# Three rearrangements in a fused two-layer kernel: combinations of B^T, two intermediates of a convolution, and column sums of W

## The chip, the cores and the metric

One core of a Trainium2 chip runs the kernel. The metric is the device time of one execution in microseconds (us). The core has five engines with a queue of their own each: TensorE (PE, matmuls), VectorE (DVE), ScalarE (ACT), GpSimd (POOL) and SyncE (SP, which here only issues transfers). An engine executes its own queue in order, and waits for the others where data or a buffer asks for it.

## The reference

All data is float32: x is 32 x 128 x 2048. Two residual layers follow each other:

```python
# layer 0: a mixture of 8 1x1 convolutions per batch entry (attention from cond), then a linear layer with 16 LoRA-like updates
att = softmax(mlp(cond));  agg_w = einsum('bk,koi->boi', att, weight);  agg_b = att @ bias_k
y = einsum('boi,bih->boh', agg_w, x) + agg_b[:, :, None]
x = x + y @ W.T + bias + sum_e coeffs[e]*scales[e] * (y @ A[e].T) @ Bf[e].T
# layer 1: a grouped 9-tap convolution along h with a context bias, then 16 small FFNs on permuted columns
z = conv1d(x, weight, groups=4) + ctx + bias
x = x + unpermute(down(gelu(up(permute(z)))))
```

The kernel folds A, B, coeffs and scales into one matrix W' = W^T + A^T B^T of 2048 x 2048, multiplies x by W' first, and mixes the channels with agg_w afterwards. The bias agg_b then appears as agg_b times the sum of each column of W'. Those 2048 column sums are called w1.

## The kernel before, in words

**Making W' and multiplying.** W' is made in 16 blocks of 128 partitions x 2048 columns (`blocks`, 4 groups of 4 kc). The first four blocks are made by `w_make` (L162): for each of four quarters, two matmuls of A^T and B^T into a PSUM bank (L172), and a DVE addition of the bank to W (L176). The other twelve are made two at a time by `w_make_two` (L205), which uses a seven-product scheme of the Strassen kind: it needs combinations of A (`a_combine`) and of B^T (`b_combine`, L193). The products are P1, P2, P6, P5, P7, P3, P4, and each is read from its bank by DVE (L213). P1, P6, P7, P4 accumulate in the same banks, so P6 can start only when DVE has read P1. `b_combine(1, ...)` runs on DVE at L873, between the first four blocks and the first `w_make_two`; `b_combine(0, ...)` runs on POOL at L912.

The large product x W' is again a seven-product scheme, two levels deep. The outer level are seven rounds (`ROUNDS`), each with eight steps g, so 56 steps i of some 24 us. Each step is a `multiply` (L316) of seven products P1, P2, P6, P5, P7, P3, P4 (L332, 4 matmuls of 128x512 each, which are 8 records), whose banks DVE or ACT adds to accumulators (L325, L327). After the first six products `between(j)`, j = 0 to 5, puts other work into the queues. POOL combines x (`x_combine`, L296 to L299) and the weights (`inner_weights`, L239 to L243) one step or round ahead.

**Buffers.** Nearly all SBUF tiles are 8 KB per partition and come from one pool of 24 slots (`slot`). A tile asks for a slot at its first use and gives it back after its last. The engine's queue waits if none is free.

**The small chain.** `small()` (L715) is a generator that is advanced once at the end of each step (L960). Steps 0 to 4 make attention weights and context biases. At step 5, when all 16 blocks are made, it makes w1: `wsum`, in which DVE and POOL have added up the blocks (128 partitions x 2048), is multiplied by a 128 x 128 matrix of ones (L801), so that each partition has the sum over all partitions; ACT copies the banks to `wbc` (L804) and SP stores the 128 x 2048 result in `w1_d` (L806). Steps 6 to 12 transform the convolution's Toeplitz weights (tiles `tw`, `t1`, L810 to L831) and store them. In the last round `late_loads` (L705) loads them and w1; `mix_begin` (L429) uses w1 on ACT.

**Last round and FFN stage.** In the last round (steps 48 to 55) and in the 128 heads of the FFN loop (L971), a pipeline over 16 pairs c of batch entries is threaded between the matmuls. Its places n go from -2 to 9; place n of pair c stands at k = 8c - 21 + n, where k < 0 are thirds of the steps of the last round and k >= 0 are heads. At each k there are three calls: `stage_first`, `stage_second` and `stage_third`. Between second and third stand one or two products of the round, or the down product of a head. The convolution is done by a scheme with six inner products per half i (i = 0 at places 4 to 6, i = 1 at places 7 to 9): `conv_inputs` (L494) makes v1 to v4 (`va`, L514, L517, L516, L518, in the code `v[0]`, `v[1]`, `v[2]`, `v[3]`) and v0, v5 (`vb`, L521 to L525) on DVE; `conv_begin` multiplies v1 and v3 at place 5 or 8, `conv_middle` v2 and v4 at place 6 or 9, `conv_end` v0 and v5. `oes`, the even and odd parts from which v1 to v4 come, live in the room of v0 and v5 in `vb`. `residual_rows` (L481) transposes the residual x in 32x32 blocks on DVE, after `conv_inputs` at places 4 and 5.

The order within a queue is that of the program text; nothing reorders it.

Of the kernel before, what the change touches and what calls it, by code (L numbers as in the profile page):

```python
# [16 lines left out]
P = 128  # L17
# [34 lines left out]
def adaln_ffn_kernel(  # L52
# [32 lines left out]
    def done(*ps):  # L85
        banks.extend(ps)
# [8 lines left out]
        for kh in range(2) for oh in range(2) for kc in range(4)  # L95
    }
    t2_d = {kc: scratch(f"t2_d{kc}") for kc in range(4)}
    w1_d = scratch("w1_d")
    tw_d = scratch("tw_d")
    te_d = scratch("te_d", (P, KEXP * P))  # L100
    ag_d = [scratch(f"ag_d{i}") for i in range(B // NCH)]
# [57 lines left out]
    def w_store(k, t):  # L159
        nc.gpsimd.dma_start(wb_d[k], t.rearrange("p k o c -> p (k o c)"))  # L160

    def w_make(k, t):  # L162

        kh, oh, kc = k
        for oi in range(2):
            for ki in range(2):
                pw = bank()

                n = QW // 2 if k == (0, 0, 0) and oi == 0 else QW
                for o0 in range(0, QW, n):  # L170
                    for c in range(2):
                        nc.tensor.matmul(  # L172
                            pw[:, o0 : o0 + n], lhsT=a_sb[kh][:, c, ki, kc],
                            rhs=bf_sb[oh][:, c, oi, o0 : o0 + n], start=(c == 0), stop=(c == 1),
                        )
                nc.vector.tensor_tensor(t[:, ki, oi], pw, t[:, ki, oi], ALU.add)  # L176
                done(pw)
        w_store(k, t)


# [12 lines left out]
    def b_combine(oh, tt):  # L193
        t = slot(f"tb_{oh}", (P, 4, QW))
        b11, b12, b21, b22 = (bf_sb[oh][:, c, oi] for c in range(2) for oi in range(2))
        tt(t[:, 0], b12, b11, ALU.subtract)
        tt(t[:, 1], b22, t[:, 0], ALU.subtract)
        tt(t[:, 2], b22, b12, ALU.subtract)
        tt(t[:, 3], b21, t[:, 1], ALU.subtract)
        return {  # L200
            "P1": b11, "P2": b21, "P3": b22, "P4": t[:, 3],
            "P5": t[:, 0], "P6": t[:, 1], "P7": t[:, 2],
        }
# [290 lines left out]
    def conv_inputs(c, i, part):  # L494
# [4 lines left out]
        low, high = xg[:, :, 0 : 2 * NM], xg[:, :, 2 * NM : 4 * NM]  # L499
        if i == 0 and part == 0:  # L500
            vb[c] = slot(f"vb_{c}", (P, 2, 2, 4 * NM))
        if part == 0:
            va[c, i] = slot(f"va_{c}{i}", (P, 4, 4 * NM))
            v = [va[c, i][:, q].rearrange("p (r m) -> p r m", r=4) for q in range(4)]

            oes = [
                vb[c][:, h].rearrange("p q (r m) -> p (q r m)", r=4).rearrange(
                    "p (r k m) -> p r (k m)", r=4, k=2
                )
                for h in (1 - i, i)  # L510
            ]
            (o0, e0), (o1, e1) = ((t[:, :, 0:NM], t[:, :, NM : 2 * NM]) for t in oes)
            stt(oes[0], low, -4.0, high, ALU.mult, ALU.add)  # L513
            tt(v[0], e0, o0, ALU.add)  # L514
            tt(oes[1], high, low, ALU.subtract)  # L515
            stt(v[2], o1, 2.0, e1, ALU.mult, ALU.add)  # L516
            tt(v[1], e0, o0, ALU.subtract)  # L517
            stt(v[3], o1, -2.0, e1, ALU.mult, ALU.add)  # L518
        else:
            v0, v5 = (vb[c][:, i, q].rearrange("p (r m) -> p r m", r=4) for q in range(2))  # L520
            stt(v0, d[1], -5.0, d[3], ALU.mult, ALU.add)  # L521
            stt(v5, d[2], -1.25, d[0], ALU.mult, ALU.add)
            w0, w5 = v0[:, :, 1:NM], v5[:, :, 0 : NM - 1]
            stt(w0, d[3][:, :, 0 : NM - 1], 4.0, w0, ALU.mult, ALU.add)
            stt(w5, d[0][:, :, 1:NM], 0.25, w5, ALU.mult, ALU.add)  # L525
# [89 lines left out]
    def stage_second(c, n):  # L615
        if n in (6, 9):
            conv_middle(c, int(n == 9))
        if n in (0, 2):
            mix_begin(2 * c + n // 2)

# [12 lines left out]
    def third_rest(c, n):  # L633
# [3 lines left out]
            residual_rows(c, 0, 0)  # L637
            residual_rows(c, 0, 1)
        if n in (4, 5, 7, 8):
            conv_inputs(c, int(n > 5), n in (5, 8))  # L640
        if n in (4, 5):
            residual_rows(c, 1, n - 4)
        if n == 8:
# [61 lines left out]
    def late_loads():  # L705
        late["tw"] = slot("tw_l", (P, 4, GR, P))
        nc.sync.dma_start(late["tw"].rearrange("p k r c -> p (k r c)"), tw_d)
        late["w1"] = slot("w1", (P, NPH, QW))
        nc.sync.dma_start(late["w1"].rearrange("p f n -> p (f n)"), w1_d)
        late["fb"] = slot("fb", (P, NPH, QW))  # L710
        nc.sync.dma_start(
            late["fb"].rearrange("p f n -> p (f n)"), fbias.to_broadcast([P, L])
# [3 lines left out]
    def small():  # L716
# [77 lines left out]

        while len(made) < 16:
            yield
        wbc = slot("wbc", (P, NPH, QW))
        for o in range(NPH):
            p5 = bank()
            for half in (slice(0, NQ), slice(NQ, QW)):  # L800
                nc.tensor.matmul(  # L801
                    p5[:, half], lhsT=ones, rhs=wsum[:, o // 2, o % 2, half], start=True, stop=True
                )
            nc.scalar.copy(wbc[:, o], p5)  # L804
            done(p5)
        nc.sync.dma_start(w1_d, wbc.rearrange("p f n -> p (f n)"))  # L806
        yield


# [51 lines left out]
    sa[0] = a_combine(0, nc.gpsimd.tensor_tensor)  # L861
    first = [wt.pop(k) for k in blocks[0:4]]

    def make_first(kc):
        t = first[kc]
        w_make(blocks[kc], t)
        made.append(blocks[kc])
        if kc == 2:
            lhs[0] = x_combine(*steps[0], xs.pop(0))
        nc.gpsimd.tensor_tensor(wsum[:, 0, 1], wsum[:, 0, 1], t[:, 0, 1], ALU.add)  # L870

    rhs = inner_weights("P1", first, make_first)
    tb[1] = b_combine(1, nc.vector.tensor_tensor)  # L873
    a_load(1, 0, 4)
    unsummed, unsummed_first = [], list(first)
    olds = {}
# [8 lines left out]
    for i, (r, g) in enumerate(steps):  # L885
# [16 lines left out]
        if ri == 0:  # L902
            ks = blocks[4 + 2 * g : 6 + 2 * g]
            if ks:
# [4 lines left out]
                    a_scale(1, 0, 4)  # L909
                    sa[1] = a_combine(1, nc.gpsimd.tensor_tensor)  # L910
                if g == 3:
                    tb[0] = b_combine(0, nc.gpsimd.tensor_tensor)  # L912
                for k, t in zip(ks, two):
                    unsummed.append((k[1], t))
                    if k[:2] == (1, 0):
# [137 lines left out]
```

## Time and profile before

| what | value |
|---|---|
| runs, median (lowest to highest) | 2639.94 us (2638.82 to 2642.12), 3 runs |
| the profiled execution | 2637.23 us, span 2635.5 us |
| granted TensorE clock, mean | 0.998 |
| L332 matmuls, seven rounds | 3136 records, 592 ns each |
| L676 and L687, FFN products | 1024 records each, 592 ns each |
| L406, mixed kernels on DVE | 158.9 us |
| L427, bias on POOL | 178.9 us |
| DMA | 609.18 MB, mean 231 GB/s |

The span is the time from the first to the last instruction that the profile shows; 1.7 us of the execution lie around it. In a timeline each line has the start, the length, the engine, the line of the code, the operation, the tiles out<-in, their shapes and the count of merged instructions; in brackets is the idle time before it and what ended it. In the list of waits stand the total, the number and the longest. A matmul of float32 shows as two records.

### The profile page before, as it was taken

How to read it: one execution, taken by the hardware profiler on the slowest of the kernel's cores; microseconds unless marked ns; L12 is line 12 of the kernel's file. 1: busy time of each engine (PE TensorE's matmuls, PEld its weight loads, DVE VectorE, ACT ScalarE, POOL GpSimd, SP SyncE). 2: the span in 40 equal slices, each digit the busy share in tenths (PEclk: the TensorE clock that was granted, in tenths of full speed). 3: DMA queues.
4: the chain of work that ended last, by engine and by line, in shares of the span. 5: the costliest groups of instructions: out<-in, count | busy, mean ns of one | idle time of the engine just before them, and what ended most of it. 6: DMA issues, size and time to landing. Idle time of an engine off the chain costs nothing.

```text
span 2635.5 us, 20243 instructions
## 1 busy us (share of the span) xinstructions
PE 2614.5 (99%) x6484; PEld 1230.3 (47%) x6484; DVE 1336.4 (51%) x2168; ACT 535.3 (20%) x1103; POOL 1230.7 (47%) x1014
## 2 busy tenths in 40 slices
PE   9999999999999999999999999999999999999998
PEld 4444444444444444444444445555455555455543
DVE  5554134344233454433366666766666666666610
ACT  0000000000000000000011144444444444444432
POOL 7321536878746644756332334434443344344222
PEclk9999999999999999999999999999999999999999
DMA  8542458788466577555667798777778777777532
GB/s 319 206 160 105 162 193 325 271 319 352 155 258 255 203 285 309 223 230 206 223 229 239 227 317 282 236 221 229 227 244 257 234 222 224 240 242 240 166 123 88
DMA packets 183610, 609.18 MB, mean 231 GB/s; under 512 B 16849, under 2 KB 88017, under 8 KB 139089
## 3 DMA queue, kind: packets, MB, share of 16 engines
q1 hardware_dynamic: 150080, 474.79, 50.6%
q0 software_dynamic: 32992, 132.14, 14.8%
q8 instruction: 52, 0.85, 0.1%
q10 hardware_dynamic: 432, 0.96, 0.1%
q14 instruction: 54, 0.43, 0.0%
HBM read 372.42 MB, written 201.85 MB: 218 GB/s over the span
## 4 chain that ended last, share of the span: by engine, by line
PE 96%; DVE 2%; DMA 1%; issue 0%; SPq 0%; POOLq 0%; ACT 0%; DVEq 0%; ACTq 0%
PE bank L332 50%; PE bank L676 16%; PE bank L687 16%; PE bank L534 6%; PE bank L442 4%; PE bank L210 2%; PE bank L172 1%; DMA xg<-x 1%; DMA ws<-in_ffw 0%; DVE vb L515 0%; DMA a_sb<-in_A 0%; DVE vb L513 0%; DVE va L514 0%; PE bank L801 0%; DVE va L516 0%
## 5 line engine op out<-in xcount | busy, mean ns | idle before, releaser
L676 PE MATMUL bank<-t,ws 128*128 128x512 f32 x1024 | 460.7, 592 | 0.6 <-DMA ws<-in_ffw 0.4
L687 PE MATMUL bank<-gl,ws 128*128 128x512 f32 x1024 | 460.2, 592 | 0.0
L694 POOL DMA_INDIRECT out<-t,orow x128 | 151.1, 1180 | 532.7 <-DVE t L692 458.6
L325 DVE TENSOR_TENSOR u<-bank,u 128x512 f32<-128x512 f32 x280 | 187.6, 688 | 415.4 <-PE bank L332 405.7
L679 ACT ACTIVATE gl<-bank 128x512 f32<-128x512 f32 x512 | 306.1, 598 | 446.4 <-PE bank L676 436.0
L332 PE MATMUL bank<-P_t,s_P 128*128 128x512 f32 x896 | 393.7, 592 | 0.0
L687 PEld LDWEIGHTS bank<-gl,ws 128*128 128x128 f32 x1024 | 194.6, 190 | 233.0 <-issue 231.5
L676 PEld LDWEIGHTS bank<-t,ws 128*128 128x128 f32 x1024 | 194.4, 190 | 227.8 <-issue 223.5
L332 PE MATMUL bank<-wo_P,s_P 128*128 128x512 f32 x640 | 281.6, 592 | 3.1 <-DVE u L325 3.1
L427 POOL TENSOR_TENSOR x<-x,fb 128x512 f32<-128x512 f32 x128 | 178.9, 1427 | 223.9 <-DMA x<-in_x 223.9
L332 PE MATMUL bank<-wo_P,xt 128*128 128x512 f32 x640 | 281.5, 592 | 0.0
L332 PEld LDWEIGHTS bank<-P_t,s_P 128*128 128x128 f32 x896 | 170.2, 190 | 213.4 <-issue 212.1
L433 ACT ACTIVATE bank<-w,aggb 128x512 f32<-128x512 f32 x128 | 80.8, 683 | 890.3 <-DVE ags L406 872.8
L692 DVE TENSOR_TENSOR t<-bank,t 128x512 f32<-128x512 f32 x128 | 88.3, 690 | 321.3 <-PE bank L687 307.7
L269 POOL TENSOR_TENSOR xt<-xt,xt 128x512 f32<-128x512 f32 x128 | 159.9, 1283 | 157.5 <-DMA xt<-in_xT 157.5
L332 PE MATMUL bank<-P_t,xt 128*128 128x512 f32 x448 | 201.4, 592 | 0.0
L325 DVE TENSOR_TENSOR p<-bank,p 128x512 f32<-128x512 f32 x112 | 77.5, 692 | 235.3 <-PE bank L332 232.1
L296 POOL TENSOR_TENSOR s_P<-xt 128x512 f32<-128x512 f32 x56 | 71.9, 1285 | 264.5 <-DMA xt<-in_xT 208.4
L332 PEld LDWEIGHTS bank<-wo_P,s_P 128*128 128x128 f32 x640 | 121.5, 190 | 155.3 <-issue 153.5
L332 PEld LDWEIGHTS bank<-wo_P,xt 128*128 128x128 f32 x640 | 121.6, 190 | 152.2 <-issue 150.2
L406 DVE SCALAR_TENSOR_TENSOR ags<-mix,att_bc,ags 128x128 f32<-128x128 f32 x224 | 158.9, 709 | 4.5
L660 POOL DMA_INDIRECT t<-hx_d,row x128 | 132.3, 1034 | 57.2 <-issue 26.0
(144 smaller groups left out, 2643.8 us busy)
## 6 DMA issues: line engine op xcount, KB each, us to landing
xt<-in_xT SPq DMA_DIRECT2D x88, 1024.0 KB
u<-u_d SPq DMA_DIRECT2D x40, 1024.0 KB
wo_P<-wb_d SPq DMA_DIRECT2D x36, 1024.0 KB
u<-c_d SPq DMA_DIRECT2D x64, 512.0 KB
x<-in_x SPq DMA_DIRECT2D x32, 1024.0 KB
xg<-x SPq DMA_DIRECT2D x256, 128.0 KB
hx_d<-x1t SPq DMA_DIRECT2D x32, 1024.0 KB
hx_d<-ht SPq DMA_DIRECT2D x32, 1024.0 KB
```

Source lines behind the costliest of these rows:

```text
L269: nc.gpsimd.tensor_tensor(out[:, i, j], a[:, i, j], b[:, i, j], op)
L325: nc.vector.tensor_tensor(to, ps, to, ALU.add)
L332: nc.tensor.matmul(ps, lhsT=lhs[k][:, bass.ts(kc, P)], rhs=rhs[k][kc], start=first and kc == 0, stop=last and kc == 3, skip_group_check=True,)
L406: nc.vector.scalar_tensor_tensor(ag, mix[:, k], att, ag, ALU.mult, ALU.add)
L427: nc.gpsimd.tensor_tensor(xt[:, f], xt[:, f], late["fb"][:, f], ALU.add)
L442: nc.tensor.matmul(pm, lhsT=ag, rhs=u[:, f], start=False, stop=True, skip_group_check=True)
L534: nc.tensor.matmul(out, lhsT=w[:, 2 * i + r], rhs=rhs, start=first and r == 0, stop=last and r == 1, skip_group_check=True,)
L660: nc.gpsimd.indirect_dma_start(out=t.rearrange("p k t -> p (k t)"), out_offset=None, in_=hx_d[g].rearrange("l k t -> l (k t)"), in_offset= ...
L676: nc.tensor.matmul(pu, lhsT=w[:, m * P : (m + 1) * P], rhs=t[:, 0], start=True, stop=True)
L679: nc.scalar.activation(gl[m], pu, AF.Gelu)
L687: nc.tensor.matmul(pd, lhsT=w[:, (MC + m) * P : (MC + m + 1) * P], rhs=gl[m], start=(m == 0), stop=(m == MC - 1),)
L694: nc.gpsimd.indirect_dma_start(out=out, out_offset=bass.IndirectOffsetOnAxis(ap=orow[:, g, h : h + 1], axis=0), in_=t[:, 1], in_offset=None,)
```

## The change

Three things are changed. (1) `conv_inputs` has three parts in place of two: v2 and v4 are made by a part of their own, which `stage_second` calls at places 5 and 8, where before they followed v3 at places 4 and 7. (2) `b_combine` returns a function that makes one of its four combinations for each call; `w_make` calls it after each of the four additions of the block kc = 3, and the call at L873 goes. On POOL, at L912, all four are still made together. (3) The products of `wsum` with ones, the ACT copies and the store of 128 equal rows go. In their place DVE transposes `wsum` in blocks of 32x32 and adds up each block's rows (128 x 64 numbers), a transfer stores them, a second one reads them back with the four groups of 32 partitions side by side in 32 partitions, DVE adds up the four and transposes, and a third transfer stores w1 as one row of 2048. These five pieces are separated by steps of the small chain, which has four steps more. `late_loads` reads w1 with a broadcast to 128 partitions. The transfers are issued from ACT's queue.

```diff
--- before.py
+++ after.py
@@ -95,7 +95,8 @@
         for kh in range(2) for oh in range(2) for kc in range(4)
     }
     t2_d = {kc: scratch(f"t2_d{kc}") for kc in range(4)}
-    w1_d = scratch("w1_d")
+    w1_d = scratch("w1_d", (1, L))
+    red_d = scratch("red_d", (P, L // GC))
     tw_d = scratch("tw_d")
     te_d = scratch("te_d", (P, KEXP * P))
     ag_d = [scratch(f"ag_d{i}") for i in range(B // NCH)]
@@ -159,7 +160,7 @@
     def w_store(k, t):
         nc.gpsimd.dma_start(wb_d[k], t.rearrange("p k o c -> p (k o c)"))
 
-    def w_make(k, t):
+    def w_make(k, t, between=lambda: None):
 
         kh, oh, kc = k
         for oi in range(2):
@@ -175,6 +176,7 @@
                         )
                 nc.vector.tensor_tensor(t[:, ki, oi], pw, t[:, ki, oi], ALU.add)
                 done(pw)
+                between()
         w_store(k, t)
 
 
@@ -193,11 +195,15 @@
     def b_combine(oh, tt):
         t = slot(f"tb_{oh}", (P, 4, QW))
         b11, b12, b21, b22 = (bf_sb[oh][:, c, oi] for c in range(2) for oi in range(2))
-        tt(t[:, 0], b12, b11, ALU.subtract)
-        tt(t[:, 1], b22, t[:, 0], ALU.subtract)
-        tt(t[:, 2], b22, b12, ALU.subtract)
-        tt(t[:, 3], b21, t[:, 1], ALU.subtract)
-        return {
+        parts = [
+            (t[:, 0], b12, b11), (t[:, 1], b22, t[:, 0]), (t[:, 2], b22, b12), (t[:, 3], b21, t[:, 1])
+        ]
+
+        def part():
+            if parts:
+                tt(*parts.pop(0), ALU.subtract)
+
+        return part, {
             "P1": b11, "P2": b21, "P3": b22, "P4": t[:, 3],
             "P5": t[:, 0], "P6": t[:, 1], "P7": t[:, 2],
         }
@@ -499,8 +505,9 @@
         low, high = xg[:, :, 0 : 2 * NM], xg[:, :, 2 * NM : 4 * NM]
         if i == 0 and part == 0:
             vb[c] = slot(f"vb_{c}", (P, 2, 2, 4 * NM))
-        if part == 0:
-            va[c, i] = slot(f"va_{c}{i}", (P, 4, 4 * NM))
+        if part < 2:
+            if part == 0:
+                va[c, i] = slot(f"va_{c}{i}", (P, 4, 4 * NM))
             v = [va[c, i][:, q].rearrange("p (r m) -> p r m", r=4) for q in range(4)]
 
             oes = [
@@ -510,12 +517,14 @@
                 for h in (1 - i, i)
             ]
             (o0, e0), (o1, e1) = ((t[:, :, 0:NM], t[:, :, NM : 2 * NM]) for t in oes)
-            stt(oes[0], low, -4.0, high, ALU.mult, ALU.add)
-            tt(v[0], e0, o0, ALU.add)
-            tt(oes[1], high, low, ALU.subtract)
-            stt(v[2], o1, 2.0, e1, ALU.mult, ALU.add)
-            tt(v[1], e0, o0, ALU.subtract)
-            stt(v[3], o1, -2.0, e1, ALU.mult, ALU.add)
+            if part == 0:
+                stt(oes[0], low, -4.0, high, ALU.mult, ALU.add)
+                tt(v[0], e0, o0, ALU.add)
+                tt(oes[1], high, low, ALU.subtract)
+                stt(v[2], o1, 2.0, e1, ALU.mult, ALU.add)
+            else:
+                tt(v[1], e0, o0, ALU.subtract)
+                stt(v[3], o1, -2.0, e1, ALU.mult, ALU.add)
         else:
             v0, v5 = (vb[c][:, i, q].rearrange("p (r m) -> p r m", r=4) for q in range(2))
             stt(v0, d[1], -5.0, d[3], ALU.mult, ALU.add)
@@ -615,6 +624,8 @@
     def stage_second(c, n):
         if n in (6, 9):
             conv_middle(c, int(n == 9))
+        if n in (5, 8):
+            conv_inputs(c, int(n == 8), 1)
         if n in (0, 2):
             mix_begin(2 * c + n // 2)
 
@@ -637,7 +648,7 @@
             residual_rows(c, 0, 0)
             residual_rows(c, 0, 1)
         if n in (4, 5, 7, 8):
-            conv_inputs(c, int(n > 5), n in (5, 8))
+            conv_inputs(c, int(n > 5), 2 * (n in (5, 8)))
         if n in (4, 5):
             residual_rows(c, 1, n - 4)
         if n == 8:
@@ -706,7 +717,7 @@
         late["tw"] = slot("tw_l", (P, 4, GR, P))
         nc.sync.dma_start(late["tw"].rearrange("p k r c -> p (k r c)"), tw_d)
         late["w1"] = slot("w1", (P, NPH, QW))
-        nc.sync.dma_start(late["w1"].rearrange("p f n -> p (f n)"), w1_d)
+        nc.sync.dma_start(late["w1"].rearrange("p f n -> p (f n)"), w1_d.to_broadcast([P, L]))
         late["fb"] = slot("fb", (P, NPH, QW))
         nc.sync.dma_start(
             late["fb"].rearrange("p f n -> p (f n)"), fbias.to_broadcast([P, L])
@@ -794,16 +805,27 @@
 
         while len(made) < 16:
             yield
-        wbc = slot("wbc", (P, NPH, QW))
+
+        wsq = slot("wsq", (P, NPH, 16, GC))
+        red, four = take(P, 4 * 16), take(GC, 4 * 4 * 16)
+        col, line = take(GC, 4 * 16), take(GC, 4 * 16)
         for o in range(NPH):
-            p5 = bank()
-            for half in (slice(0, NQ), slice(NQ, QW)):
-                nc.tensor.matmul(
-                    p5[:, half], lhsT=ones, rhs=wsum[:, o // 2, o % 2, half], start=True, stop=True
-                )
-            nc.scalar.copy(wbc[:, o], p5)
-            done(p5)
-        nc.sync.dma_start(w1_d, wbc.rearrange("p f n -> p (f n)"))
+            nc.vector.transpose(wsq[:, o].rearrange("p j c -> p (j c)"), wsum[:, o // 2, o % 2])
+            nc.vector.tensor_reduce(red[:, o * 16 : (o + 1) * 16], wsq[:, o], AX.X, ALU.add)
+        yield
+        nc.scalar.dma_start(red_d, red)
+        yield
+        nc.scalar.dma_start(
+            four.rearrange("c (g j) -> c g j", g=4), red_d.rearrange("(g c) j -> c g j", g=4)
+        )
+        yield
+        nc.vector.tensor_reduce(col, four.rearrange("c (g j) -> c j g", g=4), AX.X, ALU.add)
+        nc.vector.transpose(line, col)
+        yield
+        nc.scalar.dma_start(
+            w1_d.rearrange("u (h j c) -> (u j) h c", h=2, c=GC),
+            line.rearrange("j (h c) -> j h c", c=GC),
+        )
         yield
 
 
@@ -861,16 +883,21 @@
     sa[0] = a_combine(0, nc.gpsimd.tensor_tensor)
     first = [wt.pop(k) for k in blocks[0:4]]
 
+    part, tb[1] = b_combine(1, nc.vector.tensor_tensor)
+
     def make_first(kc):
         t = first[kc]
-        w_make(blocks[kc], t)
+
+        if kc == 3:
+            w_make(blocks[kc], t, part)
+        else:
+            w_make(blocks[kc], t)
         made.append(blocks[kc])
         if kc == 2:
             lhs[0] = x_combine(*steps[0], xs.pop(0))
         nc.gpsimd.tensor_tensor(wsum[:, 0, 1], wsum[:, 0, 1], t[:, 0, 1], ALU.add)
 
     rhs = inner_weights("P1", first, make_first)
-    tb[1] = b_combine(1, nc.vector.tensor_tensor)
     a_load(1, 0, 4)
     unsummed, unsummed_first = [], list(first)
     olds = {}
@@ -909,7 +936,9 @@
                     a_scale(1, 0, 4)
                     sa[1] = a_combine(1, nc.gpsimd.tensor_tensor)
                 if g == 3:
-                    tb[0] = b_combine(0, nc.gpsimd.tensor_tensor)
+                    part, tb[0] = b_combine(0, nc.gpsimd.tensor_tensor)
+                    for _ in range(4):
+                        part()
                 for k, t in zip(ks, two):
                     unsummed.append((k[1], t))
                     if k[:2] == (1, 0):
```

## The prediction

> **What bounds the kernel now.** First the page's busy times, then PE's waits, then, for each wait, the chain and the timeline around it.
>
> ```profile
> PE 2614.5 (99%) x6484; PEld 1230.3 (47%) x6484; DVE 1336.4 (51%) x2168; ACT 535.3 (20%) x1103; POOL 1230.7 (47%) x1014
> ```
>
> The kernel is a row of matmuls: PE is busy for 2614.5 of 2635.5 us. All that any edit can win is PE work taken out or some of the 21.0 us of PE idle, of which the waits name these:
>
> ```profile
> PE bank L210 <- DVE w L213: 4.4, 3, 3.7
> PE bank L332 <- DVE u L325: 3.1, 1, 3.1
> ...
> PE bank L534 <- DVE va L516: 0.7, 2, 0.5
> PE bank L676 <- DMA ws<-in_ffw: 0.4, 1, 0.4
> ```
>
> (Columns: total us, times, longest.) Two stand out: one of 3.7 us at L210 and one of 3.1 us at L332, both on DVE. The rest of the idle is the start (loads) and 12 us of stores after the last matmul, which the change leaves alone. The chain between 30 and 62 us shows the first:
>
> ```profile
> 35.16 0.69 DVE tb L196
> ...
> 35.88 1.64 DVE tb L197
> ...
> 39.11 1.15 DVE tb L199
> ...
> 40.77 0.69 DVE w L213
> ...
> 41.60 10.52 PE bank L210 x20
> ```
>
> PE has done the eight L210 records it can do without `tb` at 37.95 and restarts at 41.60, when DVE has made the four combinations of B^T (L196 to L199) and read the first P1 product. The first combination took 0.68 us, the next three 1.64 to 1.75, because POOL was adding beside them. The second wait, in the timeline of DVE and PE:
>
> ```profile
> 1431.23 1.64 DVE L516 SCALAR_TENSOR_TENSOR va<-vb 128x512 f32<-128x512 f32 x1
> 1432.79 1.75 DVE L517 TENSOR_TENSOR va<-vb 128x512 f32<-128x512 f32 x1
> 1434.46 0.68 DVE L518 SCALAR_TENSOR_TENSOR va<-vb 128x512 f32<-128x512 f32 x1
> 1435.06 1.41 DVE L481 STREAM_TRANSPOSE x1t<-xg 128x256 f32<-128x256 f32 x4
> 1436.40 1.24 DVE L325 TENSOR_TENSOR u<-bank,u 128x512 f32<-128x512 f32 x2
> ...
> 1432.16 1.90 PE L534 MATMUL bank<-va,tw_l 128*128 128x256 f32 x8
> ...
> 1437.19 3.67 PE L332 MATMUL bank<-wo_P,s_P 128*128 128x512 f32 x8 [3.14 <-DVE u L325]
> ```
>
> P7 adds into the bank that P6's sum (L325) must first read, and that sum stands behind v2 and v4 (L517, L518) and four transposes. Last, the products with ones, which are PE work with no wait:
>
> ```profile
> 260.57 3.62 PE L801 MATMUL bank<-wsum,small 128*128 128x256 f32 x16
> ```
>
> **What the Trainium skill says.** "SBUF — State Buffer", section "SBUF: two separate sides": VectorE and GpSimd take a shared port pair as an exclusive lock, VectorE when it has two SBUF inputs and GpSimd reads SBUF. The trace agrees nearly: at 35 to 41 us a DVE combination takes 1.7 instead of 0.68 us and a POOL addition 1.71 instead of 1.27, while L176 and L213, with one input in PSUM, stay at 0.69 beside the same POOL work. "DMA: Bandwidth & Descriptors", section "Anatomy of one DMA": about 2 us fixed per DMA; the trace has only large ones (6.1 us for a 1 MB weight store), so for a small transfer 2 us is an estimate from that page.
>
> **Part 1: the combinations one by one.** Removed: four DVE operations between L176's last sum (34.55) and L213's first (40.77). Added: the same four, each behind one of the four sums of kc = 3, which start at 29.40, 31.12, 32.84 and 34.55 with 1.03 us of DVE idle between them. A new wait: the first now needs B^T's second half by 30.09. SP's waits show one of 0.9 us at L156 for a B^T load, ahead of the weight load issued at about 29, so I take the first half as landed at 29 and the second (0.5 MB at the 430 GB/s that the windows show for 29 to 31 us, 1.2 us) at about 30.3. Behind it on DVE stand the other sums. POOL is busy from 29 to 54 us, so each combination meets the lock. If each takes 1.7 us, DVE from 30.3 does 4 x 1.7 + 3 x 0.69 = 8.9 and ends at 39.2, less the first one's shorter overlap about 38.7; PE restarts at 39.5: gain 2.1 us. But a sum from PSUM lies between two combinations, and POOL goes on during it, so the wait is shorter: POOL's 1.27 plus DVE's 0.68 minus the overlap seen (1.7 a pair) is a cycle of about 1.75 with the sum inside. Then they end at about 36.7, the first L213 at 37.4, and nothing is left of 3.65. I take 3.0, bounds 1.5 and 3.65. The banks of kc = 3 are reused by P2 and by the next product, whose sums (first, second; third, fourth) are read before. POOL loses the same 0.44 us per overlap, earlier; its L243 ends at 53.96 and P7 needs it past 65. The slot of `tb` is asked for earlier, with 18 of 24 in use: no wait. SP's order is not touched.
>
> **Part 2: W's sums.** Removed: 16 records at L801, 3.45 us of the PE chain, no wait beside them; four ACT copies and a 1 MB store on SP, both idle otherwise. Gain 3.45. Added on DVE: four transposes of 128x512 (L481 takes 0.41 us for 256 columns, so about 0.7 each) and four reductions (no row of that size; a 512-element operation is 0.68; bounds 0.5 and 1.5): 5.5 us, at most 8.8. DVE is idle from 258.0 to 271.17, and POOL from 238 to 272: hidden, and there are 4 us to spare on the middle value after the 3.45 us shift. Added on ACT's queue: three small transfers, each one step (24 us, against that page's 2) behind what it waits for; an issue costs 0.4 us, and ACT idles 3 to 10 us between copies. The 8 KB row is read with a broadcast at L709, like `fb` at L711, whose issue takes 0.97 instead of 0.86 us; ACT could use w1 at 1284.96 and PE needs it at 1304.
>
> The chain of small steps becomes four steps longer: `small` lives to step 9 instead of 5, `tw` and `t1` go from steps 6 to 12 to steps 10 to 16. I counted in the code how many of the 24 slots are alive: 24 at step 15 in the kernel before (481 to 505 us), 17 to 21 in steps 8 to 13. With `tw` and `t1` still there, step 15 wants 26, step 14 25. So two of P6_t1, P6_t2, P6_t4, p1 wait for a slot. The first that come free are p1 of step 14 (stored by about 487) and P2_t2, P2_t1 after the P6 and P5 products (491.5 and 495). POOL's L239 to L243, before at 484.2 to 504.8, then end at about 513; in the times of the kernel before (all of this moves forward together by what the earlier parts gain) PE wants the last t2 at 512 (made at 507), t's differences at 519, the next x at 529 (made at 523 to 529). Cost taken: 0; bounds 0 and 14.
>
> **Part 3: v2 and v4 later.** In the FFN stage nothing stands on DVE between the old and new place but four transposes, so only their order changes: 0. In the last round five places move. At 1342, 1372 and 1510 the move lies before no sum that a product waits for (1379.70's 0.50 us waits for v3, L516, and stays). At 1426 the sum of P6 starts where L517 did, plus the transposes: 1437.05 less 1.75 and 0.60, so P7 starts 2.35 us earlier; a transpose may take the lock's place beside POOL's last addition (ends 1433.99), so I take 2.2, bounds 1.3 and 2.4. About 0.9 us stays. Late next is P7's own sum, behind v2, v4, L521 to L525 and transposes: ready about 1440.5, product P4 needs it past 1444. The middle products need v2, v4 at 1438 and get them at 1436. At 1516.74 the last sum comes 1.2 us sooner, and with it the slot for `ws` (wait 0.44): gain 0.4, bounds 0 and 0.4.
>
> **Sum.** 3.0 + 3.45 + 2.2 + 0.4 = 9.05 us from the profiled 2637.23 (span 2635.5 and 1.7 around it): 2628.2. The median of the runs, 2639.94, stands 2.7 above the profiled one, so 2630.9. Bounds of the costs: 6.2 to 9.9 saved; with 1.5 us of spread between runs (2638.82 to 2642.12), 2628.5 to 2635.2 is this case's own range.
>
> **Rivals.** (a) The forecast: 2630.9. For it: PE is the chain everywhere and each gain is a piece of that chain with slack after it. (b) The slots give back some: POOL goes on with P6's combinations only at 506, when step 15 has ended and freed its own tiles; ten more operations of 1.3 us put the last t2 at 519 against the 512 at which PE wants it, 7 us lost: 2637.9, no change. Against: earlier frees exist. (c) Slower: P6_t2 gets the slot of `tw`, whose store is issued at the end of step 15 after a 2 us wait for DVE's last `tw` (as at L827 before), about 507.5, and at 6 us for 1 MB lands at 513.5; the same ten operations put the last t2 at 526.5: 14.5 us lost, net 2645.4. It decides once POOL goes on after 513. Against: the slots above are free sooner. (d) Part 1 and 3 do nothing, since the lock or the B^T load takes back what is gained: only 3.45, 2636.5. Against: both delays are DVE operations in front of the awaited sum, and they move.
>
> **How the numbers follow.** (a) 0.77, (b) and (d) 0.13 together, (c) 0.10. About 0.2% (5.3 us) is what a measurement here tells from no change, so faster means below 2634.7: nearly all of (a); 0.77, 0.13 and 0.10. The range is (a)'s, widened above to 2637.5 to take in half of (b) and (d).
>
> **What would show it.** After: no L801 group; the L210 wait at 38 us below 1.7 us; the L332 wait near 0.9; the POOL additions for P6 stretched to about 510 but no PE wait at 505 to 535. Wrong if PE waits there for P_t, if new waits on slots appear in the last round, where the places of tiles have moved too, or if DVE's combination waits for B^T beyond 32 us.

## The result, and the profile after

The changed kernel takes 2629.49 us in the median of 6 runs (2627.97 to 2631.55), beside 2641.85 us for the kernel before in 6 runs: the ratio is 0.9955, with a 95% interval of 0.9943 to 0.9968, or 11.9 us less. Two later comparisons of the same pair gave 0.9959 [0.9945, 0.9972] and 0.9955 [0.9942, 0.9969]. The profiled execution takes 2628.45 us with a span of 2626.7, 8.8 us less than the profiled execution of before. The medians of the three comparisons differ by 12.4, 10.2 and 11.2 us, that is 1.4 to 3.6 us more than the two profiles; what may lie behind that is told below.

The busy times of the page, and PE's waits (columns: total us, times, longest):

```profile
PE 2611.2 (99%) x6468; PEld 1228.9 (47%) x6468; DVE 1349.3 (51%) x2178; ACT 532.9 (20%) x1099; POOL 1234.8 (47%) x1014
```

```profile
PE bank L173 <- DMA bf_sb<-in_BfT: 2.1, 1, 2.1
PE bank L150 <- DVE warm L147: 1.5, 1, 1.5
PE bank L338 <- DVE u L331: 0.9, 1, 0.9
PE bank L687 <- DMA ws<-in_ffw: 0.8, 1, 0.8
PE bank L216 <- DVE w L219: 0.8, 2, 0.6
```

PE has 16 records less (6484 to 6468): the products with ones are gone. The wait of 3.7 us at the P6 product of W' (now L216) is gone, what is left under this line are two short ones. The wait of 3.1 us at P7 of the last round (now L338) has become 0.9, and the 0.7 us at the convolution's products (L534, now L543) do not appear in this profile. The wait for `ws` has grown from 0.4 to 0.8.

**Part 1** in the timelines of the changed kernel, PE first and then DVE:

```profile
37.61 3.60 PE L216 MATMUL bank<-bf_sb,a_sb 128*128 128x512 f32 x8
41.04 5.31 PE L216 MATMUL bank<-tb,sa 128*128 128x512 f32 x12
...
49.63 0.59 PE L338 MATMUL bank<-w,xt 128*128 128x512 f32 x1
```

```profile
33.27 1.09 DVE L204 TENSOR_TENSOR tb<-bf_sb 128x512 f32<-128x512 f32 x1
34.38 0.69 DVE L177 TENSOR_TENSOR w<-bank,w 128x512 f32<-128x512 f32 x1
34.98 1.05 DVE L204 TENSOR_TENSOR tb<-bf_sb,tb 128x512 f32<-128x512 f32 x1
```

Each combination (L204) now stands behind a sum (L177), as the change says, and PE goes from its eight records without `tb` to the twelve with it without a pause. The same two groups in the timeline of the kernel before:

```profile
34.35 3.60 PE L210 MATMUL bank<-bf_sb,a_sb 128*128 128x512 f32 x8
41.60 7.08 PE L210 MATMUL bank<-tb,sa 128*128 128x512 f32 x12 [3.65 <-DVE w L213]
...
51.95 7.03 PE L332 MATMUL bank<-w,xt 128*128 128x512 f32 x16
```

Two things differ from what the wait alone tells. First, the restart moved only from 41.60 to 41.04; the pause closed mainly because PE came to it later, at 37.61 plus 3.4 instead of 34.35 plus 3.4. The end of the experiments shows where that late start comes from; it is not the change. Second, the twelve records took 7.08 us before and take 5.31 now, for the same work. The stretches of the kernel before show why (the columns are the stretch; its length and PE's busy time; busy times of PEld, DVE, ACT and POOL; the granted clock; the DMA share; GB/s):

```profile
42.00:44.00 2.00, 2.00 (x5) 0.86 (x4) 1.84 (x4) 0.00 (x0) 1.93 (x3) 0.73 1.01 421
44.00:46.00 2.00, 2.00 (x4) 0.87 (x3) 0.89 (x2) 0.00 (x0) 2.00 (x2) 0.50 1.02 426
46.00:48.00 2.00, 2.00 (x5) 0.76 (x4) 1.32 (x3) 0.00 (x0) 1.84 (x3) 0.92 1.00 418
```

After the pause the granted clock was 0.50 for a while. A clock of 0.73, 0.50 and 0.92 over three stretches of 2 us is 0.54 + 1.00 + 0.16 = 1.7 us of full-speed work lost, and the group is 1.77 us longer. In the changed kernel all these stretches show 1.00. The first product with x starts 2.32 us earlier (51.95 to 49.63): 0.56 from the restart, 1.77 from the clock.

**Part 2.** DVE's new work in the changed kernel, in the timeline:

```profile
255.62 0.70 DVE L813 STREAM_TRANSPOSE wsq<-wsum 128x512 f32<-128x512 f32 x1
256.36 0.69 DVE L814 TENSOR_REDUCE small<-wsq 128x16 f32<-128x512 f32 x1
...
260.38 0.69 DVE L814 TENSOR_REDUCE small<-wsq 128x16 f32<-128x512 f32 x1
265.39 0.69 DVE L331 TENSOR_TENSOR m_P<-bank,m_P 128x512 f32<-128x512 f32 x1 [4.32 <-PE bank L338]
```

Four pairs from 255.62 to 261.07, 5.45 us, and DVE then still waits 4.32 us for PE. The longer chain holds slots of SBUF, and POOL's additions for the next round wait for them:

```profile
480.89 1.27 POOL L245 TENSOR_TENSOR P_t<-wo_P 128x512 f32<-128x512 f32 x1 [1.77 <-issue]
485.16 1.27 POOL L246 TENSOR_TENSOR P_t<-wo_P,P_t 128x512 f32<-128x512 f32 x1 [2.99 <-PE bank L338]
488.59 1.27 POOL L247 TENSOR_TENSOR P_t<-wo_P,P_t 128x512 f32<-128x512 f32 x1 [2.17 <-PE bank L338]
...
501.88 5.44 POOL L249 TENSOR_TENSOR wo_P<-wo_P 128x512 f32<-128x512 f32 x4
```

Both waits end with a product of step 15, they sum to 5.2 us, and the additions end at 507.3. In the kernel before the same additions ran from 484.19 to 504.78 without a wait; PE is 5.8 us ahead of it by then, so relative to PE the additions now end about 8 us later. No wait of PE follows. The three small transfers landed 1.4, 1.6 and 7.0 us after their issue, each with a step of 24 us to spare.

**Part 3.** DVE and then PE, in the changed kernel:

```profile
1425.10 1.64 DVE L524 SCALAR_TENSOR_TENSOR va<-vb 128x512 f32<-128x512 f32 x1
1426.66 1.41 DVE L487 STREAM_TRANSPOSE x1t<-xg 128x256 f32<-128x256 f32 x4
1428.00 0.65 DVE L331 TENSOR_TENSOR u<-bank,u 128x512 f32<-128x512 f32 x1
1428.58 0.67 DVE L526 TENSOR_TENSOR va<-vb 128x512 f32<-128x512 f32 x1
```

```profile
1428.79 3.67 PE L338 MATMUL bank<-wo_P,s_P 128*128 128x512 f32 x8 [0.87 <-DVE u L331]
```

v2 (L526) and v4 stand behind the sum that P7 waits for, and the wait is 0.87 instead of 3.14 us.

The two profiles thus add up to 2.32 + 3.45 (the removed records) + 2.27 + 0.7 (L534) - 0.4 (`ws`) = 8.3 of the 8.8 us; the other 0.5 was not traced.

### The profile page after: what moved, and what is told of

Same layout as the page of the kernel before. It is cut to its first block, busy times and chain, and to the rows that moved or that the text cites. A ratio compares the mean times of both kernels' runs of the same rounds, so it can differ in the third digit from the quotient of the medians.

```text
span 2626.7 us, 20239 instructions
## 1 busy us (share of the span) xinstructions
PE 2611.2 (99%) x6468; PEld 1228.9 (47%) x6468; DVE 1349.3 (51%) x2178; ACT 532.9 (20%) x1099; POOL 1234.8 (47%) x1014
## 4 chain that ended last, share of the span: by engine, by line
PE 98%; DVE 1%; DMA 1%; issue 0%; SPq 0%; POOLq 0%; ACT 0%; DVEq 0%; ACTq 0%
PE bank L338 51%; PE bank L687 16%; PE bank L698 16%; PE bank L543 6%; PE bank L448 4%; PE bank L216 3%; PE bank L173 1%; DMA ws<-in_ffw 0%; DVE vb L523 0%; DVE va L522 0%; DMA bf_sb<-in_BfT 0%; DVE vb L521 0%; DVE va L524 0%; DMA out<-t,orow 0%; DVE aggb L782 0%
## 5 line engine op out<-in xcount | busy, mean ns | idle before, releaser
L338 PE MATMUL bank<-P_t,s_P 128*128 128x512 f32 x896 | 393.7, 592 | 0.0
L338 PE MATMUL bank<-wo_P,s_P 128*128 128x512 f32 x640 | 281.6, 592 | 0.9 <-DVE u L331 0.9
L338 PE MATMUL bank<-wo_P,xt 128*128 128x512 f32 x640 | 281.5, 592 | 0.0
L338 PEld LDWEIGHTS bank<-P_t,s_P 128*128 128x128 f32 x896 | 170.2, 190 | 213.4 <-issue 211.2
L338 PE MATMUL bank<-P_t,xt 128*128 128x512 f32 x448 | 201.4, 592 | 0.0
L338 PEld LDWEIGHTS bank<-wo_P,s_P 128*128 128x128 f32 x640 | 121.5, 190 | 153.0 <-issue 149.7
L338 PEld LDWEIGHTS bank<-wo_P,xt 128*128 128x128 f32 x640 | 121.6, 190 | 152.2 <-issue 150.9
```

What stands on the lines that cost most here:

```text
L338: nc.tensor.matmul(ps, lhsT=lhs[k][:, bass.ts(kc, P)], rhs=rhs[k][kc], start=first and kc == 0, stop=last and kc == 3, skip_group_check=True,)
```

## The experiments

The theory after the result: each part does what was forecast, and a wait of about 3 us costs PE more than its length, since the clock may fall. Rivals: that the shorter twelve records and the surplus have another cause (the later start), and that the slots of part 2 gave something back that other parts hide.

**Each part alone**, put into the kernel before.

```diff
# p1_alone
+    part, tb[1] = b_combine(1, nc.vector.tensor_tensor)
...
+        if kc == 3:
+            w_make(blocks[kc], t, part)
...
-    tb[1] = b_combine(1, nc.vector.tensor_tensor)
# p2_alone
-                nc.tensor.matmul(
-                    p5[:, half], lhsT=ones, rhs=wsum[:, o // 2, o % 2, half], start=True, stop=True
-                )
...
+            nc.vector.transpose(wsq[:, o].rearrange("p j c -> p (j c)"), wsum[:, o // 2, o % 2])
+            nc.vector.tensor_reduce(red[:, o * 16 : (o + 1) * 16], wsq[:, o], AX.X, ALU.add)
# p3_alone
+        if n in (5, 8):
+            conv_inputs(c, int(n == 8), 1)
```

> The kernel before with part 1 alone (combinations of B^T one by one behind the four sums). Theory A (wait and clock): the 3.65 us wait at L210 goes, and with it the half-clock stretch that follows it in the kernel before (granted clock 0.50 at 44 to 46 us, 12 records in 7.08 instead of 5.31 us, 1.77 us): 5.4 us less, ratio about 0.9980. Theory B (the wait alone counts): 3.65 us less, ratio about 0.9986, and the 12 records after the place still take 7.08 us.

> The kernel before with part 2 alone (column sums by transposes and small transfers). Theory A: 3.45 us of PE work go and nothing comes for it: ratio about 0.9987; POOL's combinations for P6 end about 8 us later relative to their step, without a PE wait. Rival: the two tiles that live four steps longer make PE wait for P6's weights at the start of round P6, 5 us or more, and the ratio is 1.000 or above.

> The kernel before with part 3 alone (v2 and v4 one place later). Theory A: the 3.14 us wait at 1437 us shrinks to about 0.9, the 0.50 us wait of L534 may go: 2.3 to 2.8 us less, ratio about 0.9990. Rival: the FFN stage gives it back, with new PE waits on DVE after 1520 us: ratio 1.000.

| kernel | median us | ratio to before [95%] | as us |
|---|---|---|---|
| p1_alone | 2636.22 (21 runs) | 0.9986 [0.9979, 0.9992] | -3.7 |
| p2_alone | 2636.75 (21 runs) | 0.9987 [0.9980, 0.9994] | -3.4 |
| p3_alone | 2635.62 (21 runs) | 0.9986 [0.9980, 0.9993] | -3.7 |

(Before in the same series: 2639.72, 65 runs. The last column is the ratio's distance from 1 times this.) Each part is faster by itself, and the product of the three ratios is 0.9959: within the intervals, nothing is lost or won by putting them together. p1_alone has the ratio of its theory B (0.9986), though its twelve records took 5.39 us as theory A said: its eight records started late, at 36.16, 0.96 us of wait were left, and its restart at 40.72 came only 0.9 us sooner than in before. Part 2 gives what its removed records took, and no wait for P_t appears in its profile. Part 3 gives more than the 2.3 us that the wait lost, though its interval holds these too. The profile of p1_alone, where the P7 wait still stands, shows what may be the reason:

```profile
1434.60 6.58 PE L337 MATMUL bank<-wo_P,s_P 128*128 128x512 f32 x8 [3.15 <-DVE u L330]
```

The eight records behind the same wait of 3.1 us took 3.67 us in the profile of before, and 6.58 here: 2.9 us more in an execution in which the clock fell there.

**The wait filled**, in the kernel before: three products of 128x512 that nobody uses (the next product of the pair overwrites the bank), so that PE works during most of the wait at L210 and restarts no sooner.

```diff
         product("P2", pzs, True, True, 0, 0)
+        if ks[0] == blocks[4]:
+            for _ in range(3):
+                nc.tensor.matmul(
+                    banks[0], lhsT=sa["P1"][:, 0], rhs=tb["P1"], start=True, stop=True
+                )
```

> The kernel before with three extra matmuls of 128x512 (6 records, 2.6 us) into a free bank behind the P2 products of the first pair of blocks; their result is not used. They lie within the 3.65 us wait, which stays as long in all. Theory A (idle PE loses its clock): the half-clock stretch goes though the wait for DVE stays, 1.8 us less, ratio about 0.9993. Theory B: PE restarts at 41.6 as before and the 12 records still take 7.08 us: ratio 1.000.

The ratio is 0.9994 [0.9986, 1.0002] (2638.97 us, 13 runs), which by itself doesn't decide. Its timeline does, for this place:

```profile
34.32 3.60 PE L210 MATMUL bank<-bf_sb,a_sb 128*128 128x512 f32 x8
...
41.58 5.39 PE L210 MATMUL bank<-tb,sa 128*128 128x512 f32 x12 [1.09 <-DVE w L213]
...
50.23 7.03 PE L337 MATMUL bank<-w,xt 128*128 128x512 f32 x16
```

Same start (34.32 and 34.35), same restart (41.58 and 41.60), six records more, and yet the product with x starts 1.72 us earlier. With PE at work during the wait the clock did not fall, so the rival of the later start is out. It is one execution; all the others are put beside it at the end. The same profile lost the gain again at the P7 wait of 3.15 us, which this kernel still has. Its stretches there:

```profile
1431.24:1434.65 3.41, 1.06 (x5) 0.61 (x4) 3.41 (x6) 1.63 (x5) 1.01 (x1) 1.00 0.00 0
1434.65:1438.06 3.41, 2.61 (x3) 1.17 (x4) 3.41 (x7) 0.00 (x0) 0.00 (x0) 0.50 0.70 233
1438.06:1441.48 3.42, 3.42 (x5) 1.35 (x4) 1.57 (x5) 0.00 (x0) 0.00 (x0) 0.50 1.01 302
```

Half the clock for 6.83 us, and the eight records took 6.66 us, 3.0 more than the 3.67 of before. Minus 1.72 plus 3.0 is 1.3 us, and that is how far its span (2636.8) stands above that of before (2635.5). Whether the clock falls differs between executions: of the four profiles with this wait of 3.1 us, it fell in two (p1_alone, fill_wait) and not in the other two (before, p2_alone). With the wait of 0.9 us, it fell in none.

**The changed kernel again, and an earlier start of PE.** The changed kernel without an edit was run twice more. Two others have one or two warm-up matmuls more, to take from PE the late start that the changed kernel's profile showed.

```diff
-        for _ in range(2):
+        for _ in range(3):
```

(warm3; in warm4 it is 4.)

> The changed kernel once more, beside the next two. Theory A (each PE idle of over 3 us also risks a half-clock stretch of 3.4 us, 1.7 us lost): ratio 0.995 to 0.997, below the product 0.9959 of the three parts alone or equal to it; no half-clock stretch at 38 to 50 us or at 1420 to 1450 us in the profile. Rival (the parts simply add): 0.9959 and nothing to be seen in the clock.

> The changed kernel a third time, as the neighbour of the next two: ratio to before 0.9955 to 0.996.

> The changed kernel with three warm-up matmuls in place of two. Theory A (what is left at the start is also the clock: PE idles 1.1 to 2.1 us between warm-up and the first loads, and its first 18 records take 0.21 us each or 0.36): the idle shrinks to below 1 us and the first products of two blocks start near 34.3 in place of 37.6: about 2 us less than the changed kernel in the median, ratio to before 0.995. Rival (the start is set by the landing of the loads alone): no difference from the changed kernel.

> The changed kernel with four warm-up matmuls. Theory A: no idle left before the first products, all of them at full clock; 2 to 3 us less than the changed kernel, ratio to before 0.9945; if the warm-up outlasts the landing of B^T by more than 1 us it gives a part back. Rival: no difference, or slower by the length of the two added matmuls (1.7 to 3.4 us).

| kernel | ratio [95%] | eight records start | wait at L216 | twelve records start, take |
|---|---|---|---|---|
| changed, first | 0.9955 [0.9943, 0.9968] | 37.61 | 0 | 41.04, 5.31 |
| after_again | 0.9959 [0.9945, 0.9972] | 36.45 | 0.34 | 40.39, 5.39 |
| after_third | 0.9955 [0.9942, 0.9969] | 35.76 | 1.69 | 41.04, 5.39 |
| warm3 | 0.9960 [0.9946, 0.9973] | 34.86 | 2.42 | 40.87, 5.39 |
| warm4 | 0.9958 [0.9945, 0.9972] | 35.01 | 2.42 | 41.02, 7.08 |

No half-clock stretch follows L216 or P7 in the three profiles of the changed kernel. The earlier start gains nothing: the restart stays at about 41, and the time up to it becomes a wait. The start differs between executions in any case (p2_alone, whose code is that of before up to there, started the eight records at 36.25). What holds the restart is seen on DVE in the profile of warm3:

```profile
33.37 1.73 DVE L204 TENSOR_TENSOR tb<-bf_sb 128x512 f32<-128x512 f32 x1 [2.77 <-DMA bf_sb<-in_BfT]
35.02 0.68 DVE L177 TENSOR_TENSOR w<-bank,w 128x512 f32<-128x512 f32 x1
35.62 1.15 DVE L204 TENSOR_TENSOR tb<-bf_sb,tb 128x512 f32<-128x512 f32 x1
```

The first combination waits for the second half of B^T until 33.37, and from there it is 7.5 us to the restart at 40.87. In hold1 below the load landed at 32.16 and PE restarted at 39.63, again 7.5 us. So the new bound at this place is a load, with 7.5 us of DVE behind it. And the wait of 2.42 us, the same in both kernels, left the clock alone in warm3 and halved it in warm4:

```profile
41.02 7.08 PE L216 MATMUL bank<-tb,sa 128*128 128x512 f32 x12 [2.42 <-DVE w L219]
```

**The load earlier**, in the changed kernel: the first load of x goes behind that of B^T's second half on SP; x_later_warm3 has three warm-up matmuls as well.

```diff
-    xs = {0: [x_load(0, 0, 0)]}
     for k in blocks[2:4]:
         wt[k] = w_load(*k)
     for q in range(2):
         b_load(1, q)
+    xs = {0: [x_load(0, 0, 0)]}
```

> The changed kernel with the first load of x (1 MB) moved on SP from before the third W block to behind B^T's second half. Theory A (part 1 is now bounded by the landing of that half, at 32.2 to 33.4 us, plus 7.5 us of DVE): it lands about 2.5 us sooner, the first combination starts by 31 us and PE restarts with P6 by 38.5 instead of 39.6 to 41.0 where its start was early; with a late start nothing is gained there. 0 to 2 us less than the changed kernel. POOL's combination of x waits about 2 us for its load, without a PE wait. Rival (the lock with POOL bounds it): P6 restarts at 39.6 to 41.0 as before.

> The same with three warm-up matmuls. Theory A: the start is early each time (first products of two blocks at 34.3 to 35) and the load no longer holds P6: restart at about 38.4, 2 us before the changed kernel, no half-clock stretch, median 2 us below it, ratio to before 0.995. Rival: as the changed kernel, since a fast start only makes the wait for DVE longer.

Ratios 0.9956 [0.9942, 0.9969] and 0.9958 [0.9945, 0.9972]: no difference from the changed kernel. DVE in the profile of x_later:

```profile
35.75 1.16 DVE L204 TENSOR_TENSOR tb<-bf_sb,tb 128x512 f32<-128x512 f32 x1
36.82 0.68 DVE L219 TENSOR_TENSOR w<-bank,w 128x512 f32<-128x512 f32 x1
40.34 3.08 DVE L219 TENSOR_TENSOR w<-bank,w 128x512 f32<-128x512 f32 x5 [2.83 <-DMA w<-in_WT]
```

The combinations are done by 36.91, some 2 to 3 us earlier than in the other kernels, but the sum of the second block then waits for its W until 40.34, and PE with it to 41.08. That bound is not new. In the first profile of the changed kernel this W landed at 39.95: the moved load goes ahead of it in both orders, so the edit brings B^T's half forward (landed at 27.95 in place of 33.05) and leaves this W where it was. None of these versions beats the changed kernel.

**More slots taken**, in the changed kernel: one or two tiles that nobody uses hold a slot each from step 14 to the end of step 15, where the prediction counted 25 and 26 tiles wanted of 24.

```diff
+        if i == 14:
+            held = [slot(f"held_{n}", (P, 1)) for n in range(1)]
+            for t in held:
+                nc.vector.memset(t, 0.0)
         multiply(r, g, lhs.pop(i), rhs, olds.pop(i), between)
+        if i == 15:
+            for t in held:
+                nc.vector.tensor_scalar(t, t, 2.0, None, ALU.mult)
```

(hold1; in hold2 it is `range(2)`.)

> The changed kernel with one more of the 24 slots occupied from step 14 to the end of step 15 (a small tile that is written and scaled and not used). Theory (slots decide when P6's weights are made): P6_t4 gets its slot only at the end of step 15; the last t2 is made about 12 us later, at 511, and PE, which wants it at 506, waits about 5 us on POOL at the start of round P6: ratio to before 0.997 to 0.998. Rival (there is more slack than counted): no PE wait there, ratio as the changed kernel.

> The changed kernel with two of the 24 slots occupied from step 14 to the end of step 15 (two small tiles, written and scaled and not used). Theory (slots decide when P6's weights are made): P6_t2 and P6_t4 wait for later releases than in the run with one slot, where POOL was held up 5.9, 2.2 and 3.0 us at 478 to 492 and PE did not wait; PE waits 2 to 6 us on POOL near 506. Rival: POOL is still early enough and no PE wait appears.

hold1: 0.9960 [0.9947, 0.9974], no loss; the expectation was wrong. POOL in its profile:

```profile
483.76 1.26 POOL L245 TENSOR_TENSOR P_t<-wo_P 128x512 f32<-128x512 f32 x1 [5.85 <-PE bank L338]
487.25 1.27 POOL L246 TENSOR_TENSOR P_t<-wo_P,P_t 128x512 f32<-128x512 f32 x1 [2.24 <-PE bank L338]
491.55 1.27 POOL L247 TENSOR_TENSOR P_t<-wo_P,P_t 128x512 f32<-128x512 f32 x1 [3.02 <-PE bank L338]
```

POOL waits three times, 11.1 us, and its additions end at 510.4 instead of 507.3: PE's products free a tile every 3 to 4 us. hold2 took 2648.74 us in one run, which is beyond the range expected, and in another place. DVE, then PE, in its profile:

```profile
472.26 0.06 DVE L991 MEMSET held<- 128x1 f32 x1 [16.39 <-POOL xt L275]
```

```profile
473.14 9.46 PE L338 MATMUL bank<-P_t,s_P 128*128 128x512 f32 x16 [16.12 <-DVE p L331]
```

The second tile itself found no slot and stopped DVE for 16.4 us at the start of step 14, and PE behind it for 16.1; then 16 records took 9.46 instead of 7.03 us, since the clock stood at half until 477.90. That is the experiment's own wait: the changed kernel asks for no slot from DVE at that place. What it does show of the change comes afterwards: POOL ended its additions at 531.1, where PE's first product of the round (the 16 records `wo_P,xt`) began at 516.78. In the changed kernel these are 507.3 and 498.58. POOL was later by 5.6 us relative to PE, and PE's waits show none there.

**The windows of the clock**, read from all 14 profiles. A trace holds the times at which the granted clock changed. Within each profile they lie whole multiples of 3.413 us apart. So each execution has a fixed row of windows of this length, and PE's idle time can be added up window by window. In the kernel before, at the wait at L210 and then at the one at P7 (columns as above):

```profile
39.50:42.91 3.41, 1.31 (x3) 0.68 (x4) 3.41 (x5) 0.00 (x0) 3.25 (x3) 1.00 1.05 419
42.91:46.33 3.42, 3.42 (x5) 1.35 (x4) 2.15 (x4) 0.00 (x0) 3.40 (x4) 0.50 1.01 422
```

```profile
1432.14:1435.55 3.41, 1.91 (x9) 1.25 (x7) 3.41 (x5) 1.63 (x5) 1.85 (x2) 1.00 0.00 0
1435.55:1438.97 3.42, 1.77 (x4) 0.87 (x5) 3.42 (x8) 0.00 (x0) 0.00 (x0) 1.00 0.45 156
```

PE was idle for 2.10 us of the window up to 42.91, and the next window has half the clock. The wait at P7 lies across the end of a window and leaves 1.50 and 1.65 us in the two, and the clock stays. In the 14 profiles, from the first rise of the clock to the last matmul, it fell behind every window with 2.10 us of idle PE or more, and behind none with 1.90 or less:

| profile, place | wait | idle PE in the window with most of it | clock behind it |
|---|---|---|---|
| p2_alone, L210 | 4.66 | 2.76 | falls |
| p3_alone, L210 | 3.65 | 2.88 | falls |
| before, L210 | 3.65 | 2.10 | falls |
| warm4, L210 | 2.42 | 2.42 | falls |
| x_later, L210 | 2.22 | 2.22 | falls |
| warm3, L210 | 2.42 | 1.54 (0.87 in the window ahead) | stays |
| x_later_warm3, hold1, L210 | 1.8 | 1.79, 1.78 | stays |
| fill_wait, p1_alone, P7 | 3.15 | 2.35, 2.19 | falls |
| before, p2_alone, P7 | 3.14 | 1.65, 1.59 | stays |

(L210 stands for L216 too; in p2_alone the window ahead of its fall held 1.90.) At P7 the wait goes on for 0.8 and 1.0 us into the slow window, and a second slow one follows; at L210 PE was at work again, and one was enough.

The late start of the eight records is the same thing at the beginning of the kernel. In eight profiles, before among them, the clock first reaches its full rate between 4.3 and 5.9 us, and the eight records start between 34.3 and 35.0. In the other six, all three of the changed kernel, p1_alone, p2_alone and hold2, it does so between 10.2 and 12.8, and they start between 35.8 and 37.6. The first 16 records at L172 (L173 in the others) took 0.38 us each in before, 0.59 in the first profile of the changed kernel, and 0.55 in p2_alone, whose code is that of before up to there.

## Why the prediction was right

The forecast of 2630.9 us stands 1.4 above the 2629.49 measured, with the likeliest case (a). Its own sum was 9.05 us; the profiles give 8.8, the medians 10.2 to 12.4. Step by step:

- **PE is the chain, and each gain is a piece of it with slack after it**: right. The parts' ratios multiply to 0.9959, and the whole has 0.9955 to 0.9959.
- **Part 2, 3.45 us**: right in size (-3.4 alone). DVE's 5.45 us were foreseen as 5.5 and are hidden. The slots came free after the products named, P6 and P5 of step 15, and the cost was 0. The additions ended at 507.3, which is 513.1 in the times of before, where 513 was counted; hold2 shows at least 5.6 us of cover beyond that, so rivals (b) and (c) were further away than the text made them. The 2 us for a small transfer fits two of the three and not the third, of 8 KB, at 7.0; the section that it was taken from speaks of transfers issued from GpSimd's queue, and these go out from ACT's.
- **Part 3, 2.2 us**: the wait went from 3.14 to 0.87, as worked out (2.27 us). The term is too small all the same, since it priced a wait by its length. Where the clock falls behind it, it costs 2.9 to 3.0 us more (p1_alone, fill_wait). That happened in two of four profiles; if that is its frequency, the mean is 2.27 + 1.5 = 3.8 us, and -3.7 was measured. The frequency is an estimate from four executions (the windows say which, not how often), and the interval of p3_alone (-5.3 to -1.8) would hold the 2.3 alone too.
- **Part 1, 3.0 us**: about right in size (-3.7 alone; 2.3 to 2.9 us by the start of the first product with x in the three profiles of the changed kernel), by two errors that cancel, which is luck. The prediction had B^T's second half landed at 30.3 and PE back by 38. In the first profile of the changed kernel the first half landed at 29.33, as taken (29), and the second at 33.05: 3.7 us and not 1.2. DVE's waits for it ended at 32.2 (hold1) to 33.6 (after_third). The 1.2 us for 0.5 MB at the whole bandwidth left no room for the other loads that were under way. The sign that the text named for being wrong, DVE waiting for B^T beyond 32 us, is there in hold1, warm3, p1_alone and two of the three profiles of the changed kernel (after_again, after_third), and the bound of 1.7 us for what is left of the wait is passed in warm3, warm4 and hold1 (1.78). The restart moved by 0.6 to 1.2 us only. What made up for it is the clock, 1.7 us, of which the sum had no term. The cycle of sum and combination, taken as 1.75 us, measured 1.68 (hold1: 34.37 to 36.05).
- **0.4 us for `ws`**: wrong. The wait was 0.8, 1.0 and 0.6 us in the three profiles of the changed kernel. It was 1.1 in p2_alone, without part 3, and is absent in p3_alone and warm3. It varies by more than the term; what sets it stays open.
- **The 0.5 us at v3 (L516), said to stay**: PE's longest wait for v3 is absent from the first profile, and 0.5 and 0.9 us in the next two. It varies by as much as it is long.

So the mechanism was right in the three parts, and the term that was mis-sized is the price of a PE wait. It accounts for 1.7 us at L210 in every profile of before and of its parts that kept the whole wait, and for some 1.5 us at P7, together more than the 1.4 by which the forecast was too high; the late load took the rest back. It also fits the difference between medians and profiles: the profile of before is an execution with the early start in which the clock did not fall at P7, and lies 2.5 us under the median of the long series. That is not shown, since p2_alone's profile has no fall at P7 either and lies 0.7 us above its median.

That the clock follows PE's idle time is what the Trainium skill says in "TensorE: Matmul & The Clock Gate", section "What's actually happening": half rate after an idle window of about 3.4 us, in windows that run on their own whatever the kernel does. The traces agree in the windows: they are 3.413 us long, and their place in relation to the kernel's work differs between executions. They differ in the threshold: 2.10 us of idle PE within one window were enough (before), and 1.90 were not (p2_alone). That is why 2.42 us of waiting halved the clock in warm4 and not in warm3. No run set the place of the windows; it is read from the profiles, where the rule holds without an exception.

## What to carry to other kernels

Price a wait of the matmul engine by its length plus the clock that it may lose: here about 2 us of idle time within one window of 3.4 us cost 1.7 us more, or 2.9 to 3.0 where the wait went on into the next. Compare the duration of the same group of records ahead of and behind the wait: a longer group at an unchanged count is the sign. Where work is moved off a wait, look for the load that is now last, and read its landing from a wait that shows it, not from its size and the bandwidth. Where a side chain holds buffers longer, count for each waiting operation which product frees the next buffer: here one is freed every 3 to 4 us, which made 5 to 11 us of waiting on a side engine free of cost.

## What was not expected of the hardware

- The clock falls at the end of a window and not of a wait: in before 1.3 us after PE had gone back to work (restart at 41.60; 0.73 over 42 to 44 puts the fall at 42.9), in fill_wait while PE still waited (1434.65, restart at 1435.45). It stayed at half for 3.4 us at L210 and for 6.83 us at P7.
- Kernels that are the same up to there reach the eight records of `w_make_two` between 34.3 and 36.3 us (before, p2_alone, p3_alone and fill_wait), and the changed kernel and hold1, between 34.3 and 37.6, early or late with the first rise of the clock. In p2_alone, with the combinations still behind the sums, a start at 36.25 went with a restart at 44.51; in the changed kernel the load, which is later, hides such a delay.
- Combinations of DVE beside POOL's additions took 1.15 us each, after the first, once a sum from PSUM stood between them (hold1, warm3), where back to back they took 1.64 to 1.75 in before.
